# Splitting the last pair's sums and experts over four engines, and spacing the gathers of the other images

## The chip, the cores and the metric

The kernel runs on one core of a Trainium2 chip. A core has five engines that each work through their own instructions in order: TensorE (PE, matrix products, with its weight loads shown apart as PEld), VectorE (DVE), ScalarE (ACT), GpSimd (POOL) and SyncE (SP), which here only issues DMA transfers. Transfers are carried by 16 DMA engines that all queues share; SP, ACT and POOL can issue them. Products go to PSUM, a small memory of banks of 512 fp32 columns by 128 partitions; everything else lies in SBUF, or in HBM outside the core.

The metric is the device time of one launch, in microseconds, as the median of several runs. Before the change it is 2875.94 us (three runs, 2869.11 to 2876.08).

## The reference

Eight images of 128 channels and 32 x 32 pixels pass two layers. The first is an attention over the pixels and a spectral filter over the sequence of 1024 tokens. The second is a deformable convolution and a mixture of experts. The change touches only the second layer, cut here to its core:

```
# deformable convolution, 3 taps j; offset and mask are convolutions of the normalised image
for j in range(3):
    y  = h_grid + offset[:, 2*j];  xc = w_base + j + offset[:, 2*j + 1]
    samp = bilinear(xt, y, xc) * sigmoid(mask[:, j])      # four corners, weighted
    out  = out + einsum('bhwc,oc->bohw', samp, conv_w[:, :, 0, j])
x = x + out + conv_b
# experts: for each token the two best of eight, weighted by normalised router probabilities
t = tokens(x); h = layernorm(t)
p = softmax(h @ router_w + router_b);  top_p, top_i = top_k(p, 2);  top_p /= sum(top_p)
t = t + sum_k top_p[k] * (h @ expert_w[top_i[k]] + expert_b[top_i[k]])
```

## The kernel before

**Stages.** The attention of all eight images comes first. Then `spectral_and_second_layer` runs the spectral filter of the first layer for four pairs of images (`GROUPS`), 16 filters to a pair, and feeds the second layer of the pair before into the same instruction streams. The last pair (images 6 and 7) has no later filters to hide behind: its second layer runs alone at the end. The instruction order on each engine is the order in which the code writes the instructions; nothing is reordered.

**The planner.** The second layer of an image is a generator, `image` (L984), which writes some instructions and then yields, with the cost of what it wrote (1.0 if it gives none). In the loop over filters, each filter of a pair has eight slots: for two parities `src` and two images `m`, `filter_image` (L1411) writes one filter's products and two evacuations, the addition L1447 on DVE and the copy L1455 on ACT, and then twice some products of the filter before are written and `advance(RATE)` is called. `advance` adds `RATE` (2.85) to a budget and draws from the generators in `behind` until the budget is used up. Images of a pair are drawn one after the other. So the place of an image's instruction among the filters' instructions is decided by the sum of the costs ahead of it.

**An image in the second layer.** The tokens are turned and normalised. For each of eight tiles of 128 tokens one product with `gw` (L1016) gives the three taps' convolution of every pixel and the offsets and masks; ACT copies it to `gs`. From `gs`, 24 transfers of 256 KB write a table in HBM (`tab`, L1009), each pixel's row with its four bilinear corners beside one another, so that one gathered row of 512 floats holds all four corners. The offsets give row numbers and weights (`corners`, L936). Then `fetch` (L1054) gathers: one indirect transfer on POOL for each tile and tap, 24 to an image, into `g` (seven buffers). Four are fetched ahead, each followed by a yield of 1.3, then come two plain yields, and then 24 sums (L1080), each of four DVE operations that add a weighted corner to `x3`, each followed by a yield of 2.6. After a layer norm (`norm_steps`), a router (`gates`, L1137) picks two experts for each token; the products with all eight experts (L1098) are weighted and added into `x3` on DVE (L1104, four operations for each half of the experts), and a product turns the result back for the output (L1115, L1118).

**The last pair.** The same generator runs with `alone` set: images 6 and 7 are drawn in turn, one step each, image 7 starting `STAGGER` (16) steps later. With `alone`, every second table write is issued by ACT and not by SP, three gathers are fetched ahead, and the small operations of the layer norm's inverse square root run on DVE and not on POOL. Both images share one `gs` buffer.

The planner's loop and the sums, which the prediction's steps rest on:

Of the kernel before, what the change touches and what calls it, by code (L numbers as in the profile page):

```python
# [11 lines left out]
F32 = mybir.dt.float32  # L12
I32 = mybir.dt.int32
AF = mybir.ActivationFunctionType
ALU = mybir.AluOpType
# [3 lines left out]
P = 128  # L19
B = 8  # L20
C = 128
T = 1024
NT = T // P
HT = T // 2
# [6 lines left out]
TAPS = 3  # L31
# [1 line left out]
PHI_PAD = 127  # L33
PHI_ROW = PHI_PAD + 1 + HT
GROUPS = ((0, 1), (2, 3), (4, 5), (6, 7))
RATE = 2.85
STAGGER = 16


# [717 lines left out]
            do(*args)  # L757


def inverse_std(nc, pool, var, eps, newton):  # L760


    v = pool.tile([P, NT], F32, tag="rs_v", name="rs_v", bufs=2)
    y = pool.tile([P, NT], F32, tag="rs_y", name="rs_y", bufs=2)
    t = pool.tile([P, NT], F32, tag="rs_t", name="rs_t", bufs=2)
    bits = pool.tile([P, NT], I32, tag="rs_b", name="rs_b", bufs=2)
    nc.vector.tensor_scalar(v, var, eps, None, ALU.add)
    nc.vector.tensor_scalar(bits, v.bitcast(I32), 1, None, ALU.logical_shift_right)
    nc.vector.tensor_scalar(y.bitcast(I32), bits, -1, 0x5F3759DF, ALU.mult, ALU.add)
    newton.tensor_scalar(v, v, -0.5, None, ALU.mult)  # L770
    for _ in range(3):
        newton.tensor_mul(t, y, y)
        newton.tensor_mul(t, t, v)
        newton.tensor_scalar(t, t, 1.5, None, ALU.add)
        newton.tensor_mul(y, y, t)
    return y


def norm_steps(nc, sb, src, dst, eps, newton):


    st = sb.tile([P, NT, 6], F32, tag="st", name="st", bufs=2)
    mv = sb.tile([P, NT, 2], F32, tag="mv", name="mv", bufs=2)
    for i in range(NT):
        nc.vector.bn_stats(st[:, i, :], src[:, i, :])
        nc.vector.bn_aggr(mv[:, i, :], st[:, i, :])
        if i % 2:
            yield
    rs = inverse_std(nc, sb, mv[:, :, 1], eps, newton)
    for _ in range(3):  # L790
        yield
    for i in range(NT):
        nc.vector.tensor_scalar(
            dst[:, i, :], src[:, i, :], mv[:, i, 0:1], rs[:, i : i + 1],
            ALU.subtract, ALU.mult,
        )
        if i % 4 == 3:
            yield 1.3


class DeformAndExperts:
# [4 lines left out]
    def __init__(  # L806
        self, ctx, tc, ident, dram, conv_w, conv_b, off_w, off_b, mask_w, mask_b,
        router_w, router_b, expert_w, expert_b, out, banks,
    ):
        self.nc = tc.nc  # L810
        self.cp = ctx.enter_context(tc.tile_pool(name="d_const", bufs=1))
        self.sb = ctx.enter_context(tc.tile_pool(name="d_sb", bufs=2))
        self.ps = ctx.enter_context(tc.tile_pool(name="d_ps", bufs=banks, space=PSUM))
        self.ident, self.dram, self.out = ident, dram, out
        self.given = (
            conv_w, conv_b, off_w, off_b, mask_w, mask_b, router_w, router_b, expert_w, expert_b
        )
# [90 lines left out]
        yield  # L908

    def bank(self, name):  # L910
        return self.ps.tile([P, 512], F32, tag="ps", name=name)

    def turn_steps(self, src, dst):
# [67 lines left out]
        got.extend((idx, w))  # L981
        yield

    def image(self, b, x2, alone):  # L984
        nc, sb = self.nc, self.sb
        newton = nc.vector if alone else nc.gpsimd
        tok = sb.tile([P, NT, C], F32, tag="tok", name="tok")
        yield from self.turn_back(x2, tok)
        yield
        ht = sb.tile([P, NT, C], F32, tag="ht", name="ht")  # L990
        yield from norm_steps(nc, sb, tok, ht, 1e-6, newton)
        yield 2.0
        hc = sb.tile([C, T], F32, tag="hc", name="hc")
# [4 lines left out]

        tab = self.tabs[b % 2]
        N = TAPS * C + TAPS * 9  # L1000
        gs = sb.tile([P, NT, N], F32, tag="gs", name="gs", bufs=1)
        writes = []

        def write():
            if writes:
                i0, tap, slot, back = writes.pop(0)
                r0 = 33 - back + i0 * P
                queue = nc.scalar if alone and slot % 2 else nc.sync
                queue.dma_start(  # L1009
                    tab[tap, r0 : r0 + 4 * P, slot, :].rearrange("(i p) c -> p i c", p=P),  # L1010
                    gs[:, i0 : i0 + 4, tap * C : (tap + 1) * C],
                )

        for i in range(NT):
            pg = self.bank("p_g")
            nc.tensor.matmul(  # L1016
                pg[:, 0:N], hc[:, i * P : (i + 1) * P], self.gw, start=True, stop=True
            )
            nc.scalar.copy(gs[:, i, :], pg[:, 0:N])
            if i % 4 == 3:  # L1020
                writes += [
                    (i - 3, tap, slot, back)
                    for tap in range(TAPS) for slot, back in enumerate((0, 1, 32, 33))
                ]
            for _ in range(4 if alone else 2):
                write()
            yield
# [2 lines left out]
                write()  # L1030
            yield
        po = self.bank("p_om")
        for tap in range(TAPS):
            at = TAPS * C + 9 * tap
            nc.tensor.matmul(
                po[:, 0 : 9 * NT], self.shift[tap], gs[:, :, at : at + 9],
                start=(tap == 0), stop=(tap == TAPS - 1),
            )
        om = sb.tile([P, NT, 9], F32, tag="om", name="om")
        nc.vector.tensor_tensor(  # L1040
            om, po[:, 0 : 9 * NT].rearrange("p (i k) -> p i k", k=9), self.base, ALU.add
        )
        yield
        got = []
        yield from self.corners(om, got)
        idx, w = got
        x3 = sb.tile([P, NT, C], F32, tag="x3", name="x3")
        rows = tab.rearrange("t r s c -> (t r) (s c)")
        points = [(i, tap) for i in range(NT) for tap in range(TAPS)]
        fetched = []  # L1050

        here = []

        def fetch():  # L1054
            if len(fetched) < len(points):
                i, tap = points[len(fetched)]
                if alone:
                    at = idx[:, i, tap : tap + 1]
                else:
                    if tap == 0:  # L1060
                        here.append(sb.tile([P, TAPS], I32, tag="here", name="here", bufs=3))
                        nc.scalar.copy(here[-1], idx[:, i, :])  # L1062
                    at = here[-1][:, tap : tap + 1]
                g = sb.tile([P, 4 * C], F32, tag="g", name="g", bufs=7)
                nc.gpsimd.indirect_dma_start(  # L1065
                    out=g, out_offset=None, in_=rows,
                    in_offset=bass.IndirectOffsetOnAxis(ap=at, axis=0),
                )
                fetched.append(g)

        for n in range(3 if alone else 4):
            fetch()
            if not alone:
                yield 1.3
        yield
        yield
        for n, (i, tap) in enumerate(points):
            fetch()
            for k in range(4):
                nc.vector.scalar_tensor_tensor(  # L1080
                    x3[:, i, :], fetched[n][:, k * C : (k + 1) * C], w[:, i, tap, k : k + 1],
                    (tok if tap + k == 0 else x3)[:, i, :], ALU.mult, ALU.add,
                )
            yield 1.7 if alone else 2.6
        tt = sb.tile([P, NT, C], F32, tag="ht", name="tt")
        yield from norm_steps(nc, sb, x3, tt, 1e-5, newton)
        yield 2.0
        tc = sb.tile([C, T], F32, tag="hc", name="tc")
        yield from self.turn_steps(tt, tc)
        yield  # L1090
        got = []
# [3 lines left out]
        for i in range(NT):  # L1095
# [14 lines left out]
            if i % 4 == 3:  # L1110
# [10 lines left out]
                nc.scalar.copy(ot[:, half * 512 : half * 512 + 512], po)  # L1121
                yield
        nc.sync.dma_start(self.out[b].rearrange("c h w -> c (h w)"), ot)

    def turn_back(self, src, dst):

# [98 lines left out]
class Spectral:  # L1225
# [115 lines left out]
    def normal(self, group, newton):  # L1341

        for x1, ur in zip(group["x1"], group["ur"]):
            yield from norm_steps(self.nc, self.sb, x1, ur, 1e-5, newton)
        self.add_tiles(group)
        yield
# [127 lines left out]
def spectral_and_second_layer(tc, spec, layer, weights):  # L1474
# [27 lines left out]
    for n in range(len(work) + 1):  # L1502
        now = work[n] if n < len(work) else None
        if now is not None and now[1] == 1:
            g = now[0]
            if g:
                for m, b in enumerate(groups[g - 1]["images"]):
                    behind.append(layer.image(b, groups[g - 1]["x2"][:, m], False))
            if g + 1 < len(groups):
                starts[g + 1] = spec.begin(groups[g + 1], layer.bank)  # L1510
                behind.insert(1 if len(groups[g]["images"]) == 1 else len(behind), starts[g + 1])
# [34 lines left out]
        kept, before, pieces = sums, now, []  # L1546
    while behind:
        advance(1)
    runs = [layer.image(b, groups[-1]["x2"][:, m], True)
            for m, b in enumerate(groups[-1]["images"])]  # L1550
    alive, step = [], 0
    while runs or alive:
        if runs and step % STAGGER == 0:
            alive.append(runs.pop(0))
        alive = [r for r in alive if next(r, r) is not r]
        step += 1


@with_exitstack
# [94 lines left out]
```

## Time and profile before

| | us |
|---|---|
| median of three runs | 2875.94 |
| profiled execution, its own time | 2893.15 |
| span of the profiled execution, first to last instruction | 2891.4 |
| last spectral product `po` ends, about | 2670.8 |
| table writes of image 6 start | 2688.7 |
| first gather of image 6, of image 7 | 2713.7, 2750.2 |
| last sum of gathers, image 7, starts | 2809.3 |
| last copy of the output ends | 2887.5 |

The page gives busy time by engine, a strip of 40 slices (72 us each) with the busy share in tenths, and the clock that TensorE was granted. Further views answer for a stretch: waits (who waited for what, how long in all, how often, the longest), timelines (start, duration, engine, line, operation, and the idle time before it with what ended it), and busy time by stretch. An operation is named by what it writes and what it reads, as in `us<-pu_high,us_w`. In the stretch from 1000 to 1300, where no image of the second layer is under way, PE is busy all the time; from 1300 to 2600 it is busy 94 to 100% of each 100 us.

### The profile page before, as it was taken

The numbers are of one execution on the slowest core, as the hardware profiler recorded it, in microseconds if no ns is written. First come the engines' busy times: TensorE is split into PE (matmuls) and PEld (weight loads), VectorE is DVE, ScalarE is ACT, GpSimd is POOL, SyncE is SP. The second block draws the span as 40 slices with busy tenths as digits, with TensorE's granted clock in tenths as the row PEclk, the third lists the DMA queues.
The fourth block names the chain that finished last, engine by engine and source line by source line (L and its number), as shares of the span: only waits on it lengthen the run. The fifth ranks groups of instructions, "written<-read, shape, count | busy, mean of one in ns | idle before, by whom it ended". The sixth has DMA issues, their size and how long they took to land.

```text
span 2891.4 us, 44980 instructions
## 1 busy us (share of the span) xinstructions
PE 2666.7 (92%) x18384; PEld 1674.4 (58%) x18384; DVE 1588.8 (55%) x3146; ACT 926.5 (32%) x1246; POOL 1072.5 (37%) x1105
## 2 busy tenths in 40 slices
PE   7999999999997999999999999999999999999316
PEld 3555555555554766666666667666666666666103
DVE  4788888888885311211553643354553265353586
ACT  4676766666672111112112111212111211211100
POOL 4777777777784221111311301221311130220340
PEclk9999999999998999999999999999999999999558
DMA  1000000000002322222614410531621441530740
GB/s 27 2 16 16 2 17 16 2 16 9 16 16 58 94 67 66 73 71 51 192 44 139 128 54 30 166 90 52 190 65 50 128 121 37 163 86 29 232 117 15
DMA packets 177014, 199.80 MB, mean 69 GB/s; under 512 B 17236, under 2 KB 135188, under 8 KB 176800
## 3 DMA queue, kind: packets, MB, share of 16 engines
q1 hardware_dynamic: 147328, 134.97, 16.8%
q0 software_dynamic: 16800, 55.59, 6.1%
q10 hardware_dynamic: 12672, 6.29, 0.8%
q8 instruction: 146, 2.39, 0.3%
q14 instruction: 68, 0.56, 0.1%
HBM read 128.88 MB, written 67.92 MB: 68 GB/s over the span
## 4 chain that ended last, share of the span: by engine, by line
PE 80%; DVE 7%; issue 3%; DMA 3%; SPq 2%; POOL 2%; ACT 2%; DVEq 0%; POOLq 0%; ACTq 0%
PE pu_high L1435 18%; PE po L1406 15%; PE pu_low L1435 13%; PE s L606 9%; PE av L658 8%; PE z L627 4%; PE p_e L1098 3%; DVE x L1080 2%; PE rb L641 2%; SPq L1009 2%; DVE x L1104 1%; ACT e L611 1%; PE p_g L1016 1%; PE pq L561 1%; PE pk L575 1%
## 5 line engine op out<-in xcount | busy, mean ns | idle before, releaser
L620 POOL TENSOR_TENSOR t<-e 128x1024 f32<-128x1024 f32 x256 | 607.8, 2374 | 199.3 <-ACT e L611 199.0
L648 DVE TENSOR_TENSOR e<-e,rb 128x2048 f32<-128x2048 f32 x256 | 570.9, 2279 | 83.6 <-PE rb L641 83.6
L611 ACT ACTIVATE e<-s 128x2048 f32<-128x2048 f32 x256 | 480.9, 1879 | 252.8 <-PE s L606 250.8
L1447 DVE TENSOR_TENSOR us<-pu_high,us_w 128x512 f32<-128x512 f32 x256 | 176.9, 691 | 680.4 <-PE pu_high L1435 680.4
L1406 PE MATMUL po<-us,mf 128*128 128x128 f32 (+2 forms) x2048 | 496.1, 381 | 0.0
L1455 ACT COPY us<-pu_low 128x512 f32<-128x512 f32 x256 | 149.8, 585 | 834.6 <-PE pu_low L1435 834.6
L1279 POOL TENSOR_TENSOR diff<-teto 128x256 f32<-128x256 f32 x126 | 92.4, 739 | 854.9 <-DMA teto<-in_phi_e 758.0
L1406 PEld LDWEIGHTS po<-us,mf 128*128 128x128 f32 x2048 | 307.6, 191 | 44.8 <-issue 21.9
L606 PE MATMUL s<-q,k 32*128 32x256 f32 x4096 | 295.8, 403 | 13.6 <-ACT e L611 12.8
L658 PE MATMUL av<-e,vt 128*32 128x256 f32 x4096 | 288.7, 389 | 4.4 <-DVE e L648 3.1
L1080 DVE SCALAR_TENSOR_TENSOR x<-g,w,x 128x128 f32<-128x128 f32 x704 | 259.1, 369 | 25.2 <-DMA g<-tab,cn_idx 1.1
L606 PEld LDWEIGHTS s<-q,k 32*128 32x128 f32 x4096 | 186.2, 185 | 136.7 <-ACT e L611 115.6
L1104 DVE SCALAR_TENSOR_TENSOR x<-p_e,gates,x 128x128 f32<-128x128 f32 x512 | 177.0, 350 | 121.8 <-PE p_e L1098 104.4
L1435 PE MATMUL pu_high<-teto,ur 128*128 128x512 f32 (+1 forms) x512 | 212.6, 497 | 19.7 <-DVE us L1447 19.7
L1440 ACT COPY us_w<-pu_low 128x256 f32<-128x256 f32 x256 | 95.4, 373 | 419.2 <-PE pu_low L1435 333.4
L1065 POOL DMA_INDIRECT g<-tab,here x144 | 139.9, 972 | 236.5 <-ACT here L1062 107.8
L1435 PE MATMUL pu_low<-teto,ur 128*128 128x512 f32 (+1 forms) x512 | 186.5, 487 | 0.0
L658 PEld LDWEIGHTS av<-e,vt 128*32 128x32 f32 x4096 | 101.4, 109 | 141.8 <-issue 84.5
L1435 PEld LDWEIGHTS pu_low<-teto,sum 128*128 128x128 f32 x504 | 94.2, 191 | 108.1 <-issue 105.6
L1098 PE MATMUL p_e<-ew,tc 128*128 128x512 f32 x256 | 137.9, 639 | 16.5 <-DVE x L1104 10.0
L1435 PE MATMUL pu_low<-teto,sum 128*128 128x256 f32 x504 | 150.5, 380 | 0.7 <-ACT us L1455 0.7
L634 DVE RECIPROCAL r<-z 128x256 f32<-128x256 f32 x64 | 112.5, 1758 | 68.7 <-PE z L627 68.5
(264 smaller groups left out, 3070.0 us busy)
## 6 DMA issues: line engine op xcount, KB each, us to landing
tab<-gs SPq DMA_DIRECT2D x168, 256.0 KB
mf<-mfd SPq DMA_DIRECT2D x48, 512.0 KB
teto<-in_phi_o SPq DMA_DIRECT2D x63, 256.5 KB
teto<-in_phi_e SPq DMA_DIRECT2D x63, 256.0 KB
mfd<-mf SPq DMA_DIRECT2D x16, 512.0 KB
tab<-gs ACTq DMA_DIRECT2D x24, 256.0 KB
xc<-in_x SPq DMA_DIRECT2D x8, 512.0 KB
x1d<-xt SPq DMA_DIRECT2D x8, 512.0 KB
```

The costliest lines, as they stand in the source:

```text
L606: nc.tensor.matmul(s[:, j, c, :], img["k"][rows, hg, 2 * r + c, :], q[rows, qc * QU : (qc + 1) * QU], start=True, stop=True,)
L611: nc.scalar.activation(e.rearrange("p j c q -> p (j c q)"), s.rearrange("p j c q -> p (j c q)"), AF.Exp, scale=float(HD) ** -0.5,)
L620: nc.gpsimd.tensor_add(t, e[:, :, 0, :], e[:, :, 1, :])
L648: nc.vector.tensor_tensor(e, e, un["rb"].unsqueeze(2).to_broadcast([P, NH, 2, QU]), ALU.mult)
L658: nc.tensor.matmul(qrt["av"][32 * j : 32 * j + 32, 0:QU], img["v"][:, 2 * r + c, P * hg + 32 * j : P * hg + 32 * j + 32], un["e", r][:, j, ...
L1080: nc.vector.scalar_tensor_tensor(x3[:, i, :], fetched[n][:, k * C : (k + 1) * C], w[:, i, tap, k : k + 1], (tok if tap + k == 0 else x3)[: ...
L1098: nc.tensor.matmul(pe, tc[:, i * P : (i + 1) * P], self.ew[:, grp * 4 : grp * 4 + 4, :].rearrange("d e c -> d (e c)"), start=True, stop=True,)
L1104: nc.vector.scalar_tensor_tensor(x3[:, i, :], pe[:, k * C : (k + 1) * C], gate[:, i, grp * 4 + k : grp * 4 + k + 1], x3[:, i, :], ALU.mult ...
L1406: self.nc.tensor.matmul(out, lhsT, rhs, start=bank not in group["opened"], stop=last, skip_group_check=True)
L1435: nc.tensor.matmul(out, weights, moving, start=start, stop=stop, skip_group_check=True)
L1447: nc.vector.tensor_tensor(us[:, :, n, 2 * P :].rearrange("c two (b t) -> c two b t", b=2), high.rearrange("c two (b t) -> c two b t", b=2) ...
L1455: nc.scalar.copy(us[:, :, n, 0 : 2 * P], low)
```

## The change

It has two parts and some smaller ones.

1. `RATE` goes from 2.85 to 2.93. In `image`, the four fetches ahead are each followed by a yield of 2.0 (before 1.3), and three plain yields follow (before two).
2. `image` loses its `alone` form. Its first half becomes `points`. For the last pair a new function, `last_pair`, runs `points` for both images in turn as before, and only when both are done goes on with gathers, sums and experts in an order written out by hand. Image 7's `gs` lies in two buffers of the filters' tile `us`, so it no longer shares one with image 6, and the second layer's PSUM banks are three, where they were two.

In `last_pair`, the sums go in eight steps, four for each image, each of two tiles of tokens. `fetch` issues the six gathers of a step, into buffers of the filters' tiles, two for each tap; a step's gathers are issued two steps ahead. `weigh` multiplies the corners of tap 2 by their weights on ACT (eight operations), adds tap 0 to `tok` on DVE (eight operations) and multiplies tap 1 on DVE (one operation). `add_up` adds `tok` and the eight weighted corners by nine products with the identity into PSUM. `take` copies the sum to `x3` and takes the layer norm's statistics, `normal` normalises half an image on ACT and turns it. `expert` handles one tile: DVE adds the first four experts into `x3`, ACT weights the other four, POOL adds those up in two operations, and PE adds bias, `x3` and POOL's sum into the output. The output of an image leaves in two halves.

```diff
-RATE = 2.85
+RATE = 2.93
...
-        for n in range(3 if alone else 4):
+        for _ in range(4):
             fetch()
-            if not alone:
-                yield 1.3
-        yield
-        yield
+            yield 2.0
+        for _ in range(3):
+            yield
...
+        def fetch(img, j):
+            for tap, tag in enumerate(("x1", "ur", "mf")):
+                g = spec.sb.tile([P, 2, 4 * C], F32, tag=tag, name=f"g_{tag}", bufs=2)
+                for t in range(2):
+                    nc.gpsimd.indirect_dma_start(
...
+        def weigh(img, j):
+            w, tok = img["w"], img["tok"]
+            g = img["g"][j, 2]
+            for t in range(2):
+                for k in range(4):
+                    nc.scalar.activation(
+                        g[:, t, k, :], g[:, t, k, :], AF.Identity,
+                        scale=w[:, 2 * j + t, 2, k : k + 1],
+                    )
+            for t in range(2):
+                i = 2 * j + t
+                for k in range(4):
+                    nc.vector.scalar_tensor_tensor(
+                        tok[:, i, :], img["g"][j, 0][:, t, k, :], w[:, i, 0, k : k + 1],
+                        tok[:, i, :], ALU.mult, ALU.add,
+                    )
+            g = img["g"][j, 1]
+            nc.vector.tensor_tensor(
+                g, g, w[:, 2 * j : 2 * j + 2, 1, :].unsqueeze(3).to_broadcast([P, 2, 4, C]),
+                ALU.mult,
+            )
...
+        def add_up(img, j):
+            if j == 0:
+                img["sum"] = spec.op.tile([P, 4, 512], F32, tag="o", name="px")
+            out = img["sum"][:, j, 0 : 2 * C].rearrange("p (t c) -> p t c", c=C)
+            nc.tensor.matmul(
+                out, self.ident, img["tok"][:, 2 * j : 2 * j + 2, :], start=True, stop=False
+            )
+            for tap in (1, 2):
+                for k in range(4):
+                    nc.tensor.matmul(
+                        out, self.ident, img["g"][j, tap][:, :, k, :], start=False,
+                        stop=(tap == 2 and k == 3),
+                    )
...
+        def expert(img, i):
...
+            for grp in range(2):
+                pe.append(self.bank("p_e"))
+                nc.tensor.matmul(
+                    pe[grp], img["tc"][:, i * P : (i + 1) * P],
...
+            for k in range(4):
+                cols = slice(k * C, (k + 1) * C)
+                nc.vector.scalar_tensor_tensor(
+                    x3[:, i, :], pe[0][:, cols], gate[:, i, k : k + 1], x3[:, i, :],
+                    ALU.mult, ALU.add,
+                )
+                nc.scalar.activation(
+                    tile[:, cols], pe[1][:, cols], AF.Identity, scale=gate[:, i, 4 + k : 5 + k]
+                )
+            nc.gpsimd.tensor_add(tile[:, 4 * C : 6 * C], tile[:, 0 : 2 * C], tile[:, 2 * C : 4 * C])
+            nc.gpsimd.tensor_add(tile[:, 6 * C :], tile[:, 4 * C : 5 * C], tile[:, 5 * C : 6 * C])
...
+            nc.tensor.matmul(out, self.ebm[:, i, :], img["gt"], start=True, stop=False)
+            nc.tensor.matmul(out, x3[:, i, :], self.ident, start=False, stop=False)
+            nc.tensor.matmul(out, tile[:, 6 * C :], self.ident, start=False, stop=True)
...
+        then = {
+            2: [partial(normal, one, 0)],
+            4: [partial(normal, one, 1), partial(choose, one)],
+            5: [partial(expert, one, i) for i in range(3)],
+            6: [partial(normal, two, 0)] + [partial(expert, one, i) for i in range(3, 6)],
+            7: [partial(expert, one, i) for i in range(6, 8)],
+        }
+        fetch(*steps[0])
+        fetch(*steps[1])
+        for s, at in enumerate(steps):
+            weigh(*at)
+            if s == 4:
+                take(*steps[3])
+            add_up(*at)
+            if s + 2 < len(steps):
+                fetch(*steps[s + 2])
+            if s % 4:
+                take(*steps[s - 1])
+            for do in then.get(s, ()):
+                do()
+        take(*steps[-1])
+        normal(two, 1)
+        choose(two)
+        for i in range(NT):
+            expert(two, i)
```

`choose` runs the router (`gates`) of one image in one go.

## The prediction

> **What bounds the kernel now.** I read the page's engine shares and 40 slices first. TensorE (PE) is busy 92% of the span, and only the last slices fall off, so there are two regions: a middle that PE fills, and a tail of some 220 us (from 2671 to 2891.4) that it does not.
>
> ```profile
> PE 2666.7 (92%) x18384; PEld 1674.4 (58%) x18384; DVE 1588.8 (55%) x3146; ACT 926.5 (32%) x1246; POOL 1072.5 (37%) x1105
> ...
> PE   7999999999997999999999999999999999999316
> PEclk9999999999998999999999999999999999999558
> ```
>
> For the middle, the table of waits of PE alone (1300 to 2670) shows what still stops it, and the timelines of POOL, VectorE (DVE) and PE around 1395 show one case (start, duration, engine, line, operation; in brackets the idle time before it and what ended that):
>
> ```profile
> PE pu_high L1435 <- DVE us L1447: 31.2, 6, 6.4
> PE p_ut L1362 <- DVE ht L793: 2.3, 1, 2.3
> PE p_ut L1362 <- DVE ur L793: 2.3, 1, 2.3
> ...
> 1391.77 1.07 POOL L1065 DMA_INDIRECT g<-tab,here  x1 [15.53 <-DMA teto<-in_phi_e]
> ...
> 1386.30 0.69 DVE L1447 TENSOR_TENSOR us<-pu_high,us_w 128x512 f32<-128x512 f32 x1 [1.88 <-PE pu_high L1435]
> 1397.43 0.71 DVE L1080 SCALAR_TENSOR_TENSOR x<-g,w,tok 128x128 f32<-128x128 f32 x1 [10.44 <-DMA g<-tab,here]
> 1398.18 1.82 DVE L1080 SCALAR_TENSOR_TENSOR x<-g,w,x 128x128 f32<-128x128 f32 x3
> 1399.91 0.68 DVE L1447 TENSOR_TENSOR us<-pu_high,us_w 128x512 f32<-128x512 f32 x1
> ...
> 1389.49 1.02 PE L1435 MATMUL pu_high<-teto,ur 128*128 128x512 f32 x2
> 1400.65 2.07 PE L1435 MATMUL pu_high<-teto,ur 128*128 128x512 f32 x2 [5.39 <-DVE us L1447]
> 1408.69 1.02 PE L1435 MATMUL pu_high<-teto,ur 128*128 128x512 f32 x2
> ```
>
> Six images, six stalls. DVE sits 10.44 us in front of the first sum of gathers, because the first gather starts only when the table's writes have landed; the L1447 behind it is late, and PE's next `pu_high` with it. (The gather's wait is put down to a filter's DMA, but its own input is the table.) Filters start 5.61 us apart when undisturbed; the last three rows are 19.20 us apart where 2 x 5.61 = 11.22 belong, so this stall costs 8.0: 5.39 idle and 2.6 at a lower clock.
>
> For the tail, busy time by stretch, then the waits of ScalarE (ACT) from 2688 to 2760:
>
> ```profile
> 2714.00:2750.00 36.00, 8.68 (x18) 4.20 (x16) 27.36 (x86) 3.14 (x7) 19.51 (x19) 0.55 0.94 306
> 2750.00:2810.00 60.00, 5.65 (x24) 4.88 (x24) 52.44 (x176) 1.43 (x3) 29.32 (x32) 0.50 0.46 132
> 2820.00:2892.00 72.00, 49.03 (x149) 21.73 (x149) 49.22 (x154) 4.03 (x8) 0.00 (x0) 0.87 0.04 15
> ...
> ACT cn_m L971 <- DMA tab<-gs: 25.5, 2, 16.0
> ACT gs L1019 <- DMA tab<-gs: 5.9, 1, 5.9
> ```
>
> The columns are PE, weight loads, DVE, ACT, POOL, PE's clock, DMA share and GB/s. DVE bounds the tail (52.44 of 60 us in the sums), and the clock there is 0.50. ACT is idle but held: it issues half of the table's writes, and `cn_m` waits up to 16.0 us behind them.
>
> **What the Trainium skill says.** "TensorE: Matmul & The Clock Gate", Part 1 (what is actually happening), has the clock at half after an idle window of about 3.4 us and full again after a busy one. The trace agrees: in the 14 us around five of the stalls the mean clock is 0.76 (half rate for 2 x 0.24 x 14 = 6.7 us, two such windows), and 0.88 around the sixth and around each p_ut stall of 2.3 us (one window). The same page, Part 3 (the mechanism), says matmuls start and end in program order; the trace agrees, at 2815 p_gt had waited 14.25 us for the gates, and the p_e behind it, whose operand was copied at 2798, started right after. "ScalarE: Activation LUTs", What ACT_TABLE_LOAD costs: 186 ns + 0.833 ns an element, 93 more for each pointer operand, 93 overlapped. L104 with two pointers at 128 elements took 483 ns (186 + 107 + 186 = 479) and three came in 1.25 us, so it agrees; one pointer is then an estimated 0.39, every 0.29.
>
> **The change: the other six images.** The planner settles this. Each `advance(RATE)` is a slot; L1447 runs once per two slots, ahead of the first. From an image's start to its first sum the yields cost 37.6 up to the gathers, then 4 x 1.3 + 2 = 7.2: 44.8. 44.8 / 2.85 = 15.7, so the 16th slot, the second of its filter, and the next L1447 is behind it. After: 37.6 + 4 x 2.0 + 3 = 48.6; 48.6 / 2.93 = 16.6, the 17th slot, after the next L1447. A pair's second image (whole image 159.0, now 162.8): (159.0 + 44.8) / 2.85 = 71.5, the 72nd, again a second slot; (162.8 + 48.6) / 2.93 = 72.2, the 73rd. All six pass one L1447. Both plans end their last image in the same slot, so the density is made up.
>
> One L1447 later is 5.61 us of cover. But before the next L1447 there now stand two sums (pairs' first images) or three (second images; 211.4 + 5.2 = 216.6 is still slot 74) instead of one, each 4 x 0.37 = 1.5 us. Stalls by image, 5.4, 4.3, 6.4, 5.0, 5.1, 4.9, become 5.4 - 5.6 + 1.5 = 1.3, then 1.7 (with + 3.0), 2.3, 2.4, 1.0, 2.3: 11 us. Today's cost is 31.1 idle plus some 2.25 of half clock each, 44.6. Left: 11, and one half-rate window (about 1.7) in perhaps two or three, 4: 15. Gain 29.6; bounds 15 (the first gather lands up to 2.5 later) and 44.6 (nothing left). The `p_ut` stalls: the second layer norm's inverse moves a slot ahead, which is more than 2.3; worth 0 to 2 x (2.3 + 1.7) = 8, I take 4. POOL's filter difference now stands between gathers four and five; the fifth is wanted four sums later, so nothing. **Middle: -33.6.**
>
> **The last pair.** Old end: 2891.4. The new order puts both images' points, then all gathers and sums, into one sequence per engine.
> - Start. Image 7's copies no longer wait for `gs` (5.9), so its writes and ACT's queue, 2741.0 before, end about 2735; masks on DVE 1.6: 2736.7. Behind these stand all sums, which before began at 2717 to 2720. POOL fetches two steps' gathers meanwhile; those of image 7 (steps 4 on) wait for its table, about 2742, which is before their turn.
> - A step: DVE 8 x 0.37 + about 1.2 (1024 elements; 2048 took 2.28) = 4.2, ACT 7 x 0.29 + 0.39 = 2.4, PE 9 x 0.43 = 3.9 (a p_e of 512 columns 0.86) or 7.7 at half clock, POOL 6 x 1.26 = 7.6. Before, 24 x 1.5 = 36 us of DVE per image. Step 0 takes 7.7, steps 1 to 4 about 6.4 each with two already fetched: 2770. Image 7's sums share one PSUM tile with image 6's, so step 4 also waits for the copy of step 3, which is done by then.
> - normal and choose of image 6: 16 small DVE at 0.2, four activations 1.5, transposes and copy 1.6; then p_l 1.9, some 20 DVE at 0.25, Exp, transpose, copy: 13 in all, 2783. Step 5: 4.2.
> - An expert tile. PE takes matmuls in order, so tile i + 1's p_e stand behind tile i's last p_out: p_e 1.96, ACT 1.3, POOL 0.74 + 0.47 (rows of 256 to 1024 give 2.08 ns an element), PE 0.65, handovers 0.3: 5.4 at full clock. PE is busy 3.0 of it (1.72 + 6 x 0.22), with holes of over 2 us like those that cost p_ut a window, so some windows go cold; cold it is 7.4. I take 5.8. Before it was DVE's 2 x 1.51 = 3.0 a tile.
> - Outputs go out in halves on SP; only the last, 256 KB, is on the path.
> - Then 3 x 5.8, step 6 and normal of image 7 8, 3 x 5.8, step 7 5.2, 2 x 5.8, take, normal and choose 15, 8 x 5.8, copy and output 4: 2787.2 + 92.8 + 32.2 = 2912.2.
>
> **Tail: +21.** Bounds: +5 (5.0 a tile, start 3 earlier) and +40 (7.0 a tile).
>
> Sum: -33.6 + 21 = -12.6, on the profiled execution's 2893.15 (span 2891.4 and 1.75 around it): 2880.6. The median shown, 2875.94, lies 17.2 lower; the same difference gives 2863.3.
>
> **Rivals.** *The tail is free:* four engines share what DVE did alone (158.61 us busy of 221), ACT's pointers are cheap and tiles take 5.0. For it: DVE's share; against: the in-order chain. -33 + 5 = -28: 2848. *The clock turns it slower:* the tail's experts alternate below the busy share that keeps PE warm; 7.2 a tile puts the tail at +43, and with -33.6 it is slower by more than can be told from 7.2 up; with a middle of -28, +15: 2891. For it: 0.50 in today's sums; against: 2860 to 2890, p_e at 0.86 of 1.51 us, ran at full clock. *The stall only moves:* the first gather lands later by what the slot gives, middle -12, tail +21, +9: 2885. Against: the gathers' start is set by the writes, which keep their place.
>
> **How the numbers follow.** Likeliest 0.50 (2863, own range 2852 to 2873), free tail 0.25, cold tail 0.17, moved stall 0.08. A measurement tells 0.3%, 8.6 us, from no change. Faster: 0.32 + 0.25 = 0.57; same: 0.17 + 0.04 + 0.04 = 0.25; slower 0.18. The range reaches into both neighbours: 2843 to 2890.
>
> **What would show it.** Six L1447 stalls of 1 to 2.5 us instead of 4.3 to 6.4; no p_ut wait; the tail's first DVE sums near 2737 less the middle's gain; expert tiles 5 to 6 us apart, p_out waiting for POOL; a tail of about 240 us from the last `po`. Wrong if PE's stalls keep their length, or if the tail is under 225.

## The result and the profile after

The changed kernel takes 2905.84 us (median of four runs, 2903.23 to 2906.94), the kernel before 2876.01 beside it: a ratio of 1.0106, 95% interval 1.0087 to 1.0125. The change makes the kernel slower by some 30 us; 2863 was forecast.

The page's engine shares and the slices, as shown of before:

```profile
PE 2714.3 (94%) x18566; PEld 1711.9 (59%) x18566; DVE 1539.6 (53%) x2982; ACT 973.0 (34%) x1398; POOL 1093.6 (38%) x1137
...
PE   6999999999997999999999999999999999996465
PEclk9999999999998999999999999999999999997776
```

PE falls off earlier and the four last slices, not three, are the thin ones: the filled part became shorter, the tail longer. The last product of the spectral part (the last `po`) is the border. It ended at 2670.8 before and ends at 2630.1 now, 40.7 us earlier. From there to the end of the span it was 220.6 us and is 271.4, 50.8 longer. The table of PE's waits from 1300 to 2670 (waiting engine, tile, line, what it waited for; total, times, longest) shows what went from the middle:

```profile
PE pu_high L1634 <- DVE us L1646: 3.9, 4, 1.3
...
PE p_ut L1561 <- DVE ur L793: 0.7, 3, 0.3
...
PE p_ut L1561 <- DVE ht L793: 0.7, 3, 0.3
```

L1646 is the old L1447. Its 31.2 us of waits in six stalls are 3.9 in four, none over 1.3, and the two `p_ut` waits of 2.3 are gone. That half did what was forecast. The tail did not. First the timeline of the first two steps of image 6's sums; `px` is the PSUM tile that receives them:

```profile
2700.38 1.19 PE L1215 MATMUL px<-tok,ident 128*128 128x256 f32 x2 [19.85 <-DVE tok L1201]
...
2704.50 1.89 PE L1220 MATMUL px<-g_mf,ident 128*128 128x256 f32 x8
...
2708.39 1.89 PE L1220 MATMUL px<-g_mf,ident 128*128 128x256 f32 x8
...
2710.32 0.37 ACT L1227 COPY x<-px 128x256 f32<-128x256 f32 x1 [9.75 <-PE px L1220]
2710.72 0.29 DVE L1230 BATCH_NORM_STATS2 st<-x 128x6 f32<-128x128 f32 x1 [5.34 <-ACT x L1227]
...
2711.54 2.93 DVE L1201 SCALAR_TENSOR_TENSOR tok<-g_x,w,tok 128x128 f32<-128x128 f32 x8
```

Step 0's products end at 2706.4 (2704.50 + 1.89), step 1's at 2710.28. The copy that takes out step 0 starts at 2710.32: it has waited for step 1's products, which it does not read. Its statistics follow, and VectorE's sums of step 2 stand behind them. So the engines go round in a ring, one after the other. Then a tile of image 7's experts:

```profile
2874.61 3.57 PE L1266 MATMUL p_e<-ew,tc 128*128 128x512 f32 x4
...
2876.51 1.51 DVE L1274 SCALAR_TENSOR_TENSOR x<-p_e,gates,x 128x128 f32<-128x128 f32 x4 [4.18 <-PE p_e L1266]
...
2878.29 1.14 ACT L1278 ACTIVATE other<-p_e,gates 128x128 f32<-128x128 f32 x4 [5.40 <-PE p_e L1266]
2879.51 0.72 POOL L1281 TENSOR_TENSOR other<-other 128x256 f32<-128x256 f32 x1 [5.28 <-ACT other L1278]
2880.31 0.45 POOL L1282 TENSOR_TENSOR other<-other 128x128 f32<-128x128 f32 x1
2880.82 0.49 PE L1288 MATMUL p_out<-ident,other 128*128 128x128 f32 x2 [2.19 <-POOL other L1282]
```

The brackets say it: VectorE, ScalarE and GpSimd each idle 4.2 to 5.4 us of a tile and PE 2.2 us, waiting for the one ahead. This tile takes 6.5 us, its two `p_e` products at half clock (3.57 us; a tile at full clock has 1.88).

### The profile page after: what moved, and what is told of

Its sections match the earlier page's. It is cut to its first block, busy times and chain, and to the rows that moved or that the text cites. A ratio compares the mean times of both kernels' runs of the same rounds, so it can differ in the third digit from the quotient of the medians.

```text
span 2901.5 us, 45363 instructions
## 1 busy us (share of the span) xinstructions
PE 2714.3 (94%) x18566; PEld 1711.9 (59%) x18566; DVE 1539.6 (53%) x2982; ACT 973.0 (34%) x1398; POOL 1093.6 (38%) x1137
## 4 chain that ended last, share of the span: by engine, by line
PE 83%; DVE 6%; issue 2%; ACT 2%; POOL 2%; DMA 2%; SPq 0%; ACTq 0%; another core or an unknown queue 0%; POOLq 0%; DVEq 0%
PE pu_high L1634 18%; PE po L1605 15%; PE pu_low L1634 13%; PE s L606 9%; PE av L658 8%; PE z L627 4%; PE p_e L1109 2%; PE rb L641 2%; PE p_g L1025 2%; PE p_e L1266 1%; ACT e L611 1%; PE pq L561 1%; PE pk L575 1%; PE px L1220 1%; DVE x L1115 1%
## 5 line engine op out<-in xcount | busy, mean ns | idle before, releaser
L1646 DVE TENSOR_TENSOR us<-pu_high,us_w 128x512 f32<-128x512 f32 x256 | 176.7, 690 | 691.1 <-PE pu_high L1634 683.9
L1091 DVE SCALAR_TENSOR_TENSOR x<-g,w,x 128x128 f32<-128x128 f32 x528 | 194.8, 369 | 17.3
L1115 DVE SCALAR_TENSOR_TENSOR x<-p_e,gates,x 128x128 f32<-128x128 f32 x384 | 132.5, 350 | 98.9 <-PE p_e L1109 85.9
L634 DVE RECIPROCAL r<-z 128x256 f32<-128x256 f32 x64 | 112.5, 1757 | 69.4 <-PE z L627 69.2
L1634 PEld LDWEIGHTS pu_low<-teto,ur 128*128 128x128 f32 x512 | 97.1, 190 | 68.2 <-issue 61.2
```

Of the source, the lines that this page charges most:

```text
L1091: nc.vector.scalar_tensor_tensor(x3[:, i, :], fetched[n][:, k * C : (k + 1) * C], w[:, i, tap, k : k + 1], (tok if tap + k == 0 else x3)[: ...
L1115: nc.vector.scalar_tensor_tensor(x3[:, i, :], pe[:, k * C : (k + 1) * C], gate[:, i, grp * 4 + k : grp * 4 + k + 1], x3[:, i, :], ALU.mult ...
L1634: nc.tensor.matmul(out, weights, moving, start=start, stop=stop, skip_group_check=True)
L1646: nc.vector.tensor_tensor(us[:, :, n, 2 * P :].rearrange("c two (b t) -> c two b t", b=2), high.rearrange("c two (b t) -> c two b t", b=2) ...
```

## The experiments

They ran on four chips. On each the kernel before took 2895.6 to 2896.3 us, not 2876; every ratio below is to the kernel before on the same chip. "Behind the last po" counts from the last `po` of the same profile, so that the middle's share is out of it; "tail" is the time from there to the end of the span.

**Each part alone.** `e_middle` is the kernel before with only this:

```
-RATE = 2.85
+RATE = 2.93
...
             if not alone:
-                yield 1.3
+                yield 2.0
         yield
         yield
+        if not alone:
+            yield
```

> Only the planner's part of the change (RATE 2.93, the four yields of 2.0 and the third bare yield for the images before the last pair); the last pair stays as in the kernel before. The profiles of before and after say that the last product of the spectral part (the last po) ends 40.7 us earlier, 2670.8 to 2630.1. Theory 'the middle is what the profiles show': the last po near 2630, an unchanged tail of 221 us, a profiled span near 2851, and timed 38 to 42 us faster, about 2836. Rival 'the profile stretches the stalls': the kernel before ran 17 us longer under the profiler than its median while the changed kernel ran as long as its median, so part of the 40.7 us is the profiler's; the profiled span is again near 2851 but timed it is only 20 to 25 us faster, about 2853, and this kernel's profiled run then lies at its median.

Measured: 0.989 (0.9874 to 0.9905), 2864.37, that is 31.8 us faster; last po at 2641.3, tail 220.5. Neither number was met exactly, and the rival falls with its premise: the profiled run of before is no slower than that kernel is on these four chips. PE's waits from 1300 to 2640:

```profile
PE pu_high L1437 <- DVE us L1449: 8.2, 5, 2.4
...
PE pu_high L1437 <- DVE x L1082: 1.6, 1, 1.6
```

(L1449 is L1447 of before, L1082 a sum of gathers.) With the same planner numbers 9.8 us of these stalls are left here, where the changed kernel's profile has 3.9; the prediction had 11. `e_tail` keeps RATE 2.85, the yields of 1.3 and two bare yields, and has the new last pair.

> Only the last pair's part of the change; RATE 2.85, the yields 1.3 and the two bare yields as before. Theory 'the tail alone loses 51 us and the two parts add up': last po near 2671 in the profile, from there 271 us to the end (before 220.6), timed 48 to 53 us slower, about 2926. Under 'the profile stretches the stalls' this one is timed 48 to 53 slower as well and its profiled run lies some 17 us above its own median, since it keeps the six stalls. If the tail were slow because of something that the new planner numbers bring into it (another clock at its start, other DMA traffic), the tail here would be under 240 us.

Measured: 1.0201 (1.0187 to 1.0215), 57 us slower; last po 2675.8, tail 281.0. The six stalls are back:

```profile
PE pu_high L1634 <- DVE us L1646: 33.6, 6, 6.8
```

So the planner's numbers remove the stalls, and the tail is as slow without them. The middle gains about what was forecast, and the last pair loses more than twice what was forecast. The changed kernel itself, on two of the other chips:

> The changed kernel as it is, on the same chip as the three beside it, so that their tails can be set against its own. If the middle's 32 us gain and the tail's 57 us loss, as each was timed alone, add up: 1.008 to 1.010 of the kernel before, and a profiled tail of 271 to 281 us from the last po.

Measured: 1.0045 (1.003 to 1.0061), tail 272.1. The partner of a later run gave 1.0057 (1.004 to 1.0074), tail 274.8. The sum of the parts (+25 us) lies above these +12 and +18; the tail of `e_tail` was 6 to 9 us longer than theirs. 5 to 6 us of that lie behind the gates of image 7, where five of its tiles in a row ran at half clock (6.85 us apart where warm ones are 4.85).

**The ring of the sums.** The copy and statistics of a step go ahead of the next step's products:

```
             weigh(*at)
-            if s == 4:
-                take(*steps[3])
+            if s:
+                take(*steps[s - 1])
             add_up(*at)
...
-            if s % 4:
-                take(*steps[s - 1])
```

> The changed kernel with one line moved: the copy and the statistics of step s-1 are written ahead of the products of step s, not behind them (for step 4 they stood there already). Theory 'the step is a ring': all sums of an image stand in one PSUM tile, and the copy of step s-1 waits in the trace for the last product of step s (2710.32 is the copy of step 0, step 0's products had ended at 2706.4, step 1's at 2710.28); VectorE's next sums stand behind its statistics, so VectorE, PE and the copy run one after the other, 10 us a step where I had 6.4. With the line moved a step falls to about 6 to 7 us, six steps by about 3.5 each: 15 to 25 us faster than the changed kernel, about 2886, and the copy of step 0 starts before step 1's products end. Rival 'the clock': the steps are long because PE's products run at half rate; then the order of the copy matters little, 0 to 5 us faster, about 2903. Rival 'image 6's first normal stands in the way of step 3': also 0 to 5 here.

Measured: 1.0027 (1.0011 to 1.0043), tail 263.1. Since its partner was missing on that chip, it ran again beside the changed kernel:

> The changed kernel once more, as the partner on one chip of the run beside it. 1.004 to 1.010 of the kernel before, tail 271 to 281 us in the profile: the spread comes from the expert tiles, of which a warm one takes 4.85 us and a cold one 6.85.

> The copy of step s-1 ahead of the products of step s, now with the changed kernel on the same chip. Theory 'ring, but the gates take part of it back': in the first run of this edit the products of step 4 ended some 8 us sooner behind the last po, but the gates of image 6 only some 2.5 us sooner, and steps 5 to 7 gained another 7; so 7 to 12 us, ratio 0.0025 to 0.004 below that of its partner. Rival 'the whole 15 to 25 us that the ring was first said to cost': 0.006 to 0.008 below. Rival 'nothing but the clock's luck in the experts': under 0.0015 below.

Measured: 1.002 (1.001 to 1.0029) against 1.0057, tails 263.5 against 274.8: 11 us. From the timeline of `r_take`:

```profile
2714.01 1.89 PE L1220 MATMUL px<-g_mf,ident 128*128 128x256 f32 x8
...
2715.94 0.37 ACT L1227 COPY x<-px 128x256 f32<-128x256 f32 x1 [5.93 <-PE px L1220]
2716.34 0.29 DVE L1230 BATCH_NORM_STATS2 st<-x 128x6 f32<-128x128 f32 x1 [1.52 <-ACT x L1227]
2716.36 0.70 PE L1215 MATMUL px<-tok,ident 128*128 128x256 f32 x2 [0.46 <-ACT x L1227]
...
2717.16 2.99 DVE L1201 SCALAR_TENSOR_TENSOR tok<-g_x,w,tok 128x128 f32<-128x128 f32 x8
```

The copy now follows its own step's products at once, and step 2's sums start 77.9 us behind the last po instead of 83.0. The ring is real. Its price is neither the 15 to 25 us first expected nor the 0 to 5 of the rivals: the products of step 4 end at 111.4 instead of 116.6, but the gates of image 6 come at 124.8 and 124.9. Two waits that the changed kernel beside it has not stand in `r_take`'s table of waits from the last po on:

```profile
DVE ge L1345 <- remote: 7.8, 1, 7.8
...
ACT tc L1251 <- remote: 6.7, 1, 6.7
```

"Remote" is what the trace writes where it finds no releaser on this core. The pair is in all three kernels with this edit and the old order of work (`x_take`, `r_take`, `x_both`), while gathers are in flight. What releases them stays open. The 10 us that `r_take` has gained by image 7's gates (208.8 instead of 218.8) come from steps 5 to 7: some 7 from step 6, where image 7's first normal waited for a copy in the ring, and some 3 from expert tiles that ran warmer.

**Image 6's first normal**, in the way of step 3, moved behind step 4 (only the entry `normal(one, 0)` moves from 2 to 4 in the table `then`):

> The changed kernel with image 6's first normal (12 small VectorE operations and more, four activations, four transposes, a copy) moved from behind step 2 to behind step 4, next to its second one. Theory 'it stands in the way of step 3': in the changed kernel's trace step 3's sums begin 14.2 us after step 2's where step 4's begin 10.3 after step 3's, so steps 1 to 4 get 4 to 6 us shorter, and the chain from step 4 to the gates 2 to 4 us longer (the four activations, transposes and the copy of a half): 0 to 4 us faster in all. Rival 'normal is most of the steps' overshoot': 10 us or more faster.

Measured: 1.0068 (1.005 to 1.0086) where the changed kernel had 1.0045 on that chip, so not faster but slower by 9 us. Step 4's products end 3.5 us sooner (112.5 against 116.0), the gates come at 124.7 against 124.1: what was won in the steps is given back before the gates. The larger part of the 9 us is not shown to be this edit's: the last po lies 6.7 us later although the code ahead of it is the same, step 6 took as long as in `r_after` (21.0 us from one tile to the next), which lacks the edit, and some later tiles ran colder. The rival that this normal is most of the overshoot is refuted.

**The chain of the experts.** `expert` is cut into two, and the three `p_out` products of a tile are written behind the `p_e` products of the next:

```
-        def expert(img, i):
+        def begin(img, i):
...
+        def end(img, i):
...
+        last = []
+
+        def expert(img, i):
+            begin(img, i)
+            if last:
+                end(*last.pop())
+            last.append((img, i))
...
+        end(*last.pop())
```

> The changed kernel with the experts' tiles overlapped: the two p_e products of tile i+1, the work of VectorE, ScalarE and GpSimd on it stand ahead of the three p_out products of tile i; all instructions are the same ones. Theory 'the chain in order sets a tile's 5.8 us' (p_e, ScalarE, GpSimd, p_out, then the next p_e): a tile falls to what its busiest engine or half the chain takes, 3.0 to 4.0 us, 16 tiles by 1.8 to 2.8 each: 29 to 45 us faster than the changed kernel, about 2868. Rival 'the clock': PE is at half rate for much of a tile, and stays there; tiles fall to 5 at most, 5 to 13 us faster, about 2896.

Measured: 0.9906 (0.9891 to 0.9921), 2867.97, tail 229.3, which is 42 to 45 us below the three tails of the changed kernel. A tile in its timeline, then the busy time from 2837 to 2857 (length, PE, weight loads, VectorE, ScalarE, GpSimd, clock, DMA share, GB/s):

```profile
2844.70 1.88 PE L1266 MATMUL p_e<-ew,tc 128*128 128x512 f32 x4
...
2846.71 1.14 ACT L1278 ACTIVATE other<-p_e,gates 128x128 f32<-128x128 f32 x4 [1.26 <-PE p_e L1266]
...
2846.87 0.46 PE L1292 MATMUL p_out<-ident,other 128*128 128x128 f32 x2
...
2847.16 1.88 PE L1266 MATMUL p_e<-ew,tc 128*128 128x512 f32 x4
```

```profile
2837.00:2857.00 20.00, 18.58 (x79) 11.52 (x78) 9.83 (x28) 9.54 (x32) 9.45 (x16) 0.98 0.07 26
```

Tiles come 2.46 us apart (2844.70 to 2847.16) instead of 5.8, no `p_out` waits here, and PE is busy 93% at a clock of 0.98. The chain theory holds, and a tile fell further than it expected (3.0 to 4.0): removing the waits also removed the cold windows. The same instructions in another order are worth some 40 us (by the ratios 1.0045 and 1.0057 against 0.9906, 40 to 44). Both edits:

> Both edits tried so far at once: the copy of a step ahead of the next step's products, and the experts' tiles overlapped. Alone the first took some 20 us off the changed kernel and the second some 55. Theory 'two separate chains': the gains add up but for the part that the copy's edit won in the experts' clock, 65 to 75 us off the changed kernel, ratio 0.982 to 0.987, tail near 215 us. Rival 'one gives what the other gives': both only keep PE warm; then the ratio stays at 0.990, tail near 229.

Measured: 0.9858 (0.984 to 0.9875), tail 221.6, 7.7 us below `x_pipe`'s: the gains add, with the smaller size of the ring's.

**Searching for a better order.** `y_early` is `x_both` with image 6's first two steps written ahead of the end of image 7's table writes, which SyncE then issues alone:

> Both edits of x_both, and image 6's first two steps of sums written ahead of the end of image 7's table writes and corners (image 7's writes then all on SyncE's queue). The first VectorE sums of the changed kernel start 67.2 us behind the last po because ScalarE issues image 7's writes (16.6 us for the last six) and the mask stands behind them; in the kernel before image 6's sums started some 47 us behind it. Theory 'the start is worth what it is late': sums start 47 to 52 us behind the last po and the tail ends 8 to 15 us ahead of x_both's. Rival 'gathers and writes share the DMA': gathers of image 6 land late under image 7's writes, and image 7's table is complete later on one queue, so its own gathers wait: 0 to 4 us gained, or a loss.

Measured: 0.9855 (0.9834 to 0.9875), the same as `x_both`; tail 223.4. First sums at 45.9, gates of image 6 at 124.3 where `x_both` has 123.8: nothing gained, as the rival said. What was won at the start was lost to image 7's table: its writes start 63.9 us behind the last po instead of 40.8, because the products and copies ahead of them now stand behind image 6's steps, and image 6's third step starts at 82.5 instead of 77.8.

`z_order` is `x_both` with another table `then` and with experts between the instructions of image 7's gates:

```
-            2: [partial(normal, one, 0)],
-            4: [partial(normal, one, 1), partial(choose, one)],
-            5: [partial(expert, one, i) for i in range(3)],
-            6: [partial(normal, two, 0)] + [partial(expert, one, i) for i in range(3, 6)],
-            7: [partial(expert, one, i) for i in range(6, 8)],
+            3: [partial(normal, one, 0)],
+            4: [partial(normal, one, 1)],
+            5: [partial(choose, one)],
+            6: [partial(expert, one, 0), partial(normal, two, 0)],
+            7: [partial(expert, one, 1)],
...
-        choose(two)
+        choose(two, [partial(expert, one, i) for i in range(2, 8)])
```

> x_both with the last pair's order changed and nothing else: image 6's first normal behind step 3, its gates (choose) behind step 5, and six of image 6's eight expert tiles placed between the instructions of image 7's gates; image 7's first normal behind step 6. Theory 'what is left of the tail is engines idle behind gates': in x_both's trace PE does next to nothing from step 4's products to the gates of image 6 (some 14 us) and again from step 7's products to the gates of image 7 (some 15 us); with the experts of image 6 in the second hole and step 5 in the first, the tail falls from 222 us to about 195, ratio 0.975 to 0.979. Rival 'the gates' chain is stretched by what is put into it' (VectorE does 1.5 us for each expert tile put between two instructions of the gates): 0 to 8 us gained, ratio 0.983 to 0.986.

Measured: 0.9861 (0.9846 to 0.9877), no faster than `x_both` by the ratio, with a tail 7 us shorter (214.8): the rival again. The gates of image 7 come at 182.1 (189.2 in `x_both`), but with six tiles put between their instructions they take 28.2 us from the last copy of the sums instead of 15.3. `z_sp` is `z_order` with image 7's writes taken off ScalarE's queue:

```
-                queue = nc.scalar if alone and slot % 2 else nc.sync
+                queue = nc.scalar if alone and slot % 2 and len(parts) == 1 else nc.sync
```

> z_order, and image 7's 24 table writes all issued by SyncE instead of half of them by ScalarE. In the changed kernel ScalarE is held 16.6 us by its last six issues, and image 7's mask and through it all VectorE sums stand behind them, 66 to 67 us behind the last po. Theory 'ScalarE's queue sets the start': first sums at about 50 us behind the last po, and the end comes 8 to 15 us ahead of z_order's. Rival 'the table is the limit, not the queue': image 7's own gathers cannot start before its writes have landed, so what image 6's sums win is lost waiting at step 4, as it was in y_early (sums 20 us earlier, the gates at the same place): 0 to 4 us.

Measured: 0.9786 (0.9772 to 0.9799), 2834.32, the fastest of all, faster than both kernels. First sums at 49.7, tail 205.7. Of the 21 us to `z_order`, 9 are in the tail, as the theory has it; 11 lie before the last po (2627.0 against 2638.1), where the code is the same.

## Why the prediction was wrong

The forecast summed -33.6 in the middle and +21 in the tail on the profiled 2893.15, giving 2880.6. The profiled run of after took 2903.23: 22.7 more. The middle was 7.1 better than forecast, the tail 29.8 worse.

**The middle was right.** A first sum that falls behind one more L1447 is what removes the stalls: the six of before, and of `e_tail`, became 1.3 us at most in the changed kernel's first profile and 2.4 at most in any profile with the new planner numbers, and the `p_ut` waits went too. The gain is 31.8 us timed alone, 40.7 in the pair of profiles. In the eleven other profiles with the new planner numbers the last po ended between 2627.0 and 2641.3, so its size is uncertain by some 7 us either way, whatever the last pair does; with that spread, it is partly luck that the forecast of 33.6 lies so near 31.8. The rivals that the stall only moves and that the tail is free are both refuted, by these stalls and by the 50.8 us.

**The tail, term by term** (us; "forecast" are the prediction's terms, "measured" the changed kernel's profile):

| term | forecast | measured |
|---|---|---|
| last po to the first sums | 65.9 | 67.2 |
| steps 0 to 4 | 33.3 | 49.9 |
| rest of normal and gates of image 6 | 13 | 8.2 |
| step 5 | 4.2 | 8.9 |
| three tiles | 17.4 | 18.3 |
| step 6, first normal of image 7 | 8 | 12.5 |
| three tiles | 17.4 | 18.2 |
| step 7 | 5.2 | 5.9 |
| two tiles | 11.6 | 11.5 |
| take, normal, gates of image 7 | 15 | 16.0 |
| eight tiles | 46.4 | 46.5 |
| last copy, output, end | 4 | 8.3 |
| sum | 241.4 | 271.4 |

The step that failed is "Step 0 takes 7.7, steps 1 to 4 about 6.4 each with two already fetched". It let VectorE, PE and the copy overlap as if each step only waited for data. I saw that image 7's sums share a PSUM tile with image 6's and thought of that one place, step 4; the copies of all other steps were written behind the next step's products and waited for them. So 33.3 became 49.9. In the trace the sums of steps 2, 3 and 4 start 10.3, 14.2 and 12.3 us after those of the step before. Undoing the ring gives back 5 us up to step 4's products and 11 in all; moving the normal gives 3.5 there. If the two add up, that is about half of the 16.6. Parts of normal were counted once in the steps and once in the 13, which gave 4.8 back; the rest is not shown by any single edit. Once the steps fetched ahead are used up, a step waits for GpSimd's six gathers, 6 x 1.26 = 7.6: in `z_order` the sums of steps 2 and 3 start 7.55 apart, not 6.4, and ScalarE's weighing in both waits for a gather to land:

```profile
2719.46 2.45 ACT L1194 ACTIVATE g_mf<-g_mf,w 128x128 f32<-128x128 f32 x8 [4.85 <-DMA g_mf<-tab,cn_idx]
...
2727.51 2.49 ACT L1194 ACTIVATE g_mf<-g_mf,w 128x128 f32<-128x128 f32 x8 [5.35 <-DMA g_mf<-tab,cn_idx]
```

Step 5 was priced in the same way: its 4.2 us are VectorE's alone, and PE's products run on for 5.1 us after VectorE is done (2759.24 to 2764.34). In step 6's excess of 4.5 us stands the ring again.

**The start, the tile and the queue were right.** First sums at 67.2 for 65.9; ScalarE's last six writes held `cn_m` 16.7 us. A tile took 5.9 on average (94.5 us for sixteen, 92.8 forecast), in a mixture of warm and cold ones. That was the costly part, and its reason the chain in program order: "TensorE: Matmul & The Clock Gate" of the Trainium skill, Part 3 (the mechanism), states that matmuls start and end in program order, and here, with only that order changed, the tile fell to 2.46. The rival that the clock makes the kernel slower had the direction right, but its tiles of 7.2 did not come. Of the 3.0 us that I gave PE for a tile at full clock it used 2.3 (93% of 2.46). One reading of the prediction was too strong: the `p_ut` waits of 2.3 us are shorter than the idle window that it sets them beside, and still the mean clock around them was 0.88. That short waits can cost clock is what the lines show; how long PE must idle for it they do not.

**The end** costs 4 us more than forecast. From the waits of SyncE's queue, before and then after:

```profile
SPq L1650 <- DMA out<-ot: 1.9, 1, 1.9
SPq L1650 <- PEq L1650: 0.7, 2, 0.5
```

```profile
SPq L1844 <- PEq L1844: 5.3, 2, 4.7
SPq L1844 <- DMA out<-ot: 1.1, 1, 1.1
```

The output lands sooner, in halves, but the last thing waited for is PE's sequencer, 4.7 us instead of 0.5. Every run with the new last pair shows 4.4 to 4.7 too, `e_middle` 0.5. No run tells why.

**The step from the profile to the median** failed as well: "The median shown, 2875.94, lies 17.2 lower; the same difference gives 2863.3". The changed kernel's median is 2.6 us above its profiled run, which with the 17.2 makes another 19.8 of error: 42.5 in all with the 22.7. The experiments suggest where the 17.2 came from: on their four chips the kernel before has a median of 2896, near its profiled 2893.15, so the profile and the first median seem to stand for two different levels of the kernel before. The changed kernel shows no such gap: 2906 in the first comparison, 2909 and 2914 in two others. On those two the change costs 12 and 18 us, not 30. That the kernel before varies because its six stalls hang on when gathers land would fit, but no profile of a 2876 us run exists, so this is open.

## What to carry to other kernels

When work is shared out over more engines, write down for each engine the order of the instructions and ask of every copy out of a shared PSUM tile, and of every product that closes a chain, what has been written ahead of it; the sum of busy times says nothing here. The remedy was twice an order: the take of one step ahead of the next step's products (11 us), the next tile's products ahead of this tile's last ones (some 40 us). And compare a profiled run with the median of the same comparison before a difference between them is carried over to another kernel.

## What the runs showed that I had not expected

- A chain's idle holes cost twice: tiles overlapped ran at clock 0.98 and 2.46 us apart, against 5.8 at a mean of 0.77 (2847 to 2893 in the changed kernel).
- ACT and VectorE waits of 5 to 8 us marked "remote" appear while gathers run: two in each of the three kernels with the earlier copy and the old order, one in `y_early`, none in `z_order` and `z_sp`. Their cause is open.
- The same middle, in twelve profiles whose programs differ only in the last pair, ended within 14.3 us (2627.0 to 2641.3), 0.5% of the span; the changed kernel alone, in three profiles, at 2630.1, 2633.2 and 2636.7. A difference of that size between two programs need not come from the lines that differ. It goes with PE's waits for VectorE in front of `pu_high` (1300 to 2620): 1.0 to 3.9 us in the three profiles that end first (`z_sp`, `y_early`, the changed kernel's first), 6.3 to 9.8 in the nine that end at 2633.2 or later. Why the same code stalls more in one program than in another is open.
